# Attention output with the values stationary in 32 columns per head, normalised between two block transposes

## The chip, the cores and the metric

The kernel runs on one core of a Trainium2 chip. A core has five engines that run their own instruction streams and wait for one another through semaphores: TensorE (PE, matrix products; its weight loads are shown apart as PEld), VectorE (DVE), ScalarE (ACT), GpSimd (POOL) and SyncE (SP, which here issues the DMA transfers). Matrix products write to PSUM, which has eight banks per partition; everything else is in SBUF. The metric is the device time of one execution in microseconds (us). A profile of one execution gives every instruction's start and length.

## The reference

One layer of cross-attention and one feed-forward layer, each behind a layer norm and with a residual, for 2 batches of 1024 tokens of 256 numbers, all in float32. The context has 77 keys per batch, and there are 16 heads of 16 dimensions:

```
q = layernorm(x) @ Wq + bq        k = ctx @ Wk + bk        v = ctx @ Wv + bv
att = softmax(0.25 * q k^T * mask - 1e10 * (1 - mask))     over the 77 keys, per head
x   = x + (att v) @ Wo + bo
t   = layernorm(x)
x   = x + layernorm(t + relu(t @ w1 + b1) @ w2 + b2) * gamma + beta
```

The feed-forward layer has 8 experts in the reference, but the routing weights are set to the constant row (1, 0, ..., 0), so that only expert 0 (256 to 1024 to 256) enters the output.

## The kernel before, in words

Tokens go in eight halves of 256, and a half is two tiles of 128 tokens; there are 16 tiles. The stages of several halves are emitted interleaved. Products that carry the weights keep float32's accuracy by splitting each operand into a high and a low part of type float32r and summing three products (`up` line 573, `dn` line 602, `pq` line 404, `px1` line 531). The products of the softmax's numerators with the values are plain float32 ones, and a float32 product is two passes on TensorE, each with its own weight load.

For one tile the attention runs like this:

- scores for four heads at a time on TensorE (line 433) and the mask's factor on VectorE (line 444), into `u`, 128 tokens by 16 x 77 numbers;
- the mask's bias on GpSimd (line 453), the maximum per head (line 458) and its subtraction (line 462) on VectorE;
- the 1232 columns (head, key) of `u` are cut into ten chunks of 128 (the last has 80), regardless of where heads end, and each chunk is turned by TensorE against an identity matrix (`s_turn`, line 469), four to a PSUM bank;
- ScalarE takes the exponential out of that bank into `pT` (`s_exp`, lines 477 and 480);
- ten output products (`s_out`, line 487): the turned chunk is stationary, and 68 columns stream past it: the values of four heads with a column of ones after each, laid out in `vb` so that the rows of a chunk meet their own head's values and zeros elsewhere. All ten sum into one PSUM bank `po`, tokens on partitions;
- the column of ones gives the sum per head; VectorE takes its reciprocal (line 499) and multiplies (line 501) into `o` (`s_norm`).

The layout `vb` is made at the start: the values with bias go to `v_sb` (line 311), and 25 small DMA transfers, issued on SP's queue, place the pieces of heads in their chunks (`v_place`, stage `vp`). Both buffers are filled by GpSimd first (lines 251 and 253).

For a half, `o` of the two tiles is turned on TensorE (`o_turn`, stage `pot`, line 515), split into high on ScalarE (`o_hi`, line 519) and low on VectorE (`o_lo`, line 523), and projected (`px1`).

The order is not written by hand: the class `Stages` holds each stage with its engine, an estimated length, what it needs, a rank, and the ring of buffers it takes from; `order()` is a list scheduling over these numbers, and the stages are emitted in the order that comes out. Each engine then works through its own stream in that order. So an estimated length or a ring that changes also moves other stages. PSUM's eight banks are shared out as scores 2, turned chunks 1, general 3, feed-forward 2.

Of the kernel before, what the change touches and what calls it, by code (L numbers as in the profile page):

```python
"""Cross-attention layer and feed-forward layer, each behind a layer norm, on one NeuronCore.

The reference sets the routing weights to the constant one-hot row (1, 0, ..., 0), so the output is
the one of expert 0: the router and the experts behind weight 0 do not enter it.

Matrix products keep float32's accuracy: an operand x is split exactly into hi + lo, where hi is x
rounded to float32r (12 significant bits) and lo = x - hi fits float32r as well, and a product is
hi*hi + hi*lo + lo*hi with float32 sums. The scores stack hi and lo along the contraction, the
products with the softmax's numerators are float32 ones.

Tokens go in halves of 256: token 256 h + 2 p + n is in partition p, tile n. The stages of three
halves are emitted interleaved, so that the tensor engine has the feed-forward layer of one half
to do while the softmax of the next one runs on the other engines.
"""
# [12 lines left out]
AF = mybir.ActivationFunctionType  # L27
# [25 lines left out]
class Stages:  # L53
    """Stages of the computation, each on one engine, and the order to emit them in.

    A stage has the engine, a weight (its length), the stages it needs, a rank (the lower, the more
    urgent), and, where it takes a buffer of a ring, the ring, its size and the buffer's last readers.
    """
# [7 lines left out]
    def hop(self, k, u):  # L66
        """From the end of a stage to the start of one that needs it"""
        if k[0] == u[0]:
            return 0.0
        return {"VP": 0.26, "SS": 0.15, "VV": 0.13, "SV": 0.15, "VG": 0.16, "VS": 0.13, "GV": 0.07, "QP": 2.2, "QS": 2.2, "QV": 2.2}.get(  # L70
            self.all[k]["eng"] + self.all[u]["eng"], 0.2
        )

    def order(self):
        """List scheduling: whenever an engine is free, its most urgent stage that can start."""
# [59 lines left out]
def chunk_heads(T):  # L135
    """Rows (head, key) in chunks of 128: first of four heads, its own heads from and to, its rows"""
    out = []
    for r0 in range(0, H * T, P):
        r1 = min(r0 + P, H * T)
        out.append((min(r0 // T, H - 4), r0 // T, (r1 - 1) // T + 1, r1 - r0))  # L140
    return out


@with_exitstack
def layer(ctx: ExitStack, tc: tile.TileContext, a: dict, out: bass.AP):
# [6 lines left out]
    heads = chunk_heads(T)  # L152
    NCH = len(heads)
# [26 lines left out]
    # the activation table, before the first loads are here  # L180
    warm = const([P, 1], "warm")
    # the tensor engine's clock likewise
    zero = const([P, 512], "zero", mybir.dt.bfloat16)
# [4 lines left out]
    def warm_up(i):  # L188
        pw = bank(ps_s, f"pw{i}")
        nc.tensor.matmul(pw, lhsT=zero[:, :P], rhs=zero, start=True, stop=True)  # L190
# [59 lines left out]
    vb = const([P, B, NCH, 4, D + 1], "vb")  # L250
    nc.gpsimd.memset(vb, 0.0)
    v_sb = const([T, B, H, D + 1], "v_sb")
    nc.gpsimd.memset(v_sb, 1.0)
# [56 lines left out]
    def v_bias(b):  # L310
        nc.vector.tensor_tensor(
            v_sb[:, b, :, :D],
# [5 lines left out]
    # the pieces of the heads in the chunks of 128 rows  # L318
    pieces = []
    for c, (h0, ha, hb, r) in enumerate(heads):  # L320
        for h in range(ha, hb):
            r0, r1 = max(h * T, c * P), min((h + 1) * T, c * P + r)
            pieces.append((c, h, h - h0, r0, r1))

    def v_place(c, h, k, r0, r1):
        load(vb[r0 - c * P : r1 - c * P, :, c, k], v_sb[r0 - h * T : r1 - h * T, :, h])

# [1 line left out]
    sts = {}  # L329

    def stats(src, name):
        """mean and variance + eps of tiles of tokens"""
# [64 lines left out]
    def a_query(h):  # L397
        # Group g = 2 c + j holds heads 4 g .. 4 g + 3: one half of the partitions hi, the other lo.
# [65 lines left out]
    def s_turn(h, n, s):  # L464
        uf = us[h, n].rearrange("p h t -> p (h t)")
        pt = pss["t", h, n, s] = bank(ps_t, f"pp{h}_{n}_{s}", (P, 4, P))
        for c in range(4 * s, min(4 * s + 4, NCH)):
            r = heads[c][3]
            nc.tensor.transpose(pt[:r, c - 4 * s], uf[:, c * P : c * P + r], ident)  # L469

    def s_exp(h, n, s):
        if s == 0:
            pTs[h, n] = work([P, NCH, P], "pT", f"pT{h}_{n}", RINGS["pT"])
        pT, pt = pTs[h, n], pss.pop(("t", h, n, s))
        c0, c1 = 4 * s, min(4 * s + 4, NCH)
        full = c1 if heads[c1 - 1][3] == P else c1 - 1
        nc.scalar.activation(pT[:, c0:full], pt[:, : full - c0], AF.Exp)  # L477
        if full < c1:
            r = heads[full][3]
            nc.scalar.activation(pT[:r, full], pt[:r, full - c0], AF.Exp)  # L480
# [351 lines left out]
```

## Time and profile before

| what | us |
|---|---|
| median of three runs (239.4 to 240.75) | 239.61 |
| span of the profiled execution, first to last instruction | 237.8 |
| TensorE busy / its weight loads | 217.8 / 205.7 |
| VectorE busy | 185.9 |
| GpSimd busy | 155.3 |
| ScalarE busy | 126.0 |

The profiled execution's own time is known by its span, 237.8 us; the median of the runs lies 1.8 us above it. In the lines of the profile, L487 is line 487 of the kernel, `out<-in` names the tiles, xN is a count, and "idle before" is time that the engine stood still ahead of that group, with what ended it. The slices cut the span into 40 equal parts and give the busy share of each in tenths. The chain is followed back from the last instruction to whatever released it, so that it names the work that set the end. Matmuls are pipelined and their ends are modelled, so the lengths of neighbouring matmuls overlap; the distance between starts is the better price.

### The profile page before, as it was taken

The numbers are of one execution on the slowest core, as the hardware profiler recorded it, in microseconds if no ns is written. First come the engines' busy times: TensorE is split into PE (matmuls) and PEld (weight loads), VectorE is DVE, ScalarE is ACT, GpSimd is POOL, SyncE is SP. The second block draws the span as 40 slices with busy tenths as digits, with TensorE's granted clock in tenths as the row PEclk, the third lists the DMA queues.
The fourth block names the chain that finished last, engine by engine and source line by source line (L and its number), as shares of the span: only waits on it lengthen the run. The fifth ranks groups of instructions, "written<-read, shape, count | busy, mean of one in ns | idle before, by whom it ended". The sixth has DMA issues, their size and how long they took to land.

```text
span 237.8 us, 4535 instructions
## 1 busy us (share of the span) xinstructions
PE 217.8 (92%) x1726; PEld 205.7 (86%) x1727; DVE 185.9 (78%) x385; ACT 126.0 (53%) x268; POOL 155.3 (65%) x131
## 2 busy tenths in 40 slices
PE   8799788799997899799999999999999999999980
PEld 3589567698996798799999999999999999999970
DVE  2378998999999999999987789997962473727544
ACT  2369952635573676564465737625375365274510
POOL 5048899976988468683728976668254557575641
PEclk9869958999999999999999999999999999999997
DMA  6991001500000000000000001000010001001011
GB/s 181 335 373 19 10 7 36 193 3 0 4 0 0 3 0 0 21 28 3 0 0 3 1 3 44 0 3 0 3 45 0 3 0 47 34 10 46 2 44 44
DMA packets 8875, 9.19 MB, mean 39 GB/s; under 512 B 3321, under 2 KB 6039, under 8 KB 8855
## 3 DMA queue, kind: packets, MB, share of 16 engines
q1 hardware_dynamic: 8855, 8.92, 11.7%
q8 instruction: 13, 0.21, 0.4%
q14 instruction: 7, 0.06, 0.1%
HBM read 6.65 MB, written 2.10 MB: 37 GB/s over the span
## 4 chain that ended last, share of the span: by engine, by line
PE 59%; DVE 30%; POOL 3%; ACT 2%; DMA 2%; issue 2%; SPq 0%; DVEq 0%
PE py L602 17%; PE pz L573 14%; PE po L487 8%; DVE u L444 5%; DVE u L462 5%; PE pp L469 5%; PE px L531 4%; DVE mx L458 3%; PE s L433 3%; DVE qs L422 3%; PE pq L404 3%; DMA wq<-in_L_xattn_Wq 2%; PE pk L290 2%; POOL w1l L266 2%; PE py L547 1%
## 5 line engine op out<-in xcount | busy, mean ns | idle before, releaser
L591 POOL TENSOR_TENSOR hl<-h,hh 128x512 fp32r<-128x512 f32 x32 | 42.7, 1337 | 25.1 <-ACT hh L587 24.0
L453 POOL TENSOR_TENSOR u<-u,mb 128x616 f32<-128x616 f32 x32 | 46.7, 1465 | 13.7 <-DVE u L444 10.1
L582 ACT ACTIVATE h<-pz,cols 128x256 f32<-128x256 f32 x64 | 26.8, 470 | 31.3 <-PE pz L573 30.2
L487 PE MATMUL po<-vb,pT 128*128 128x68 f32 (+1 forms) x320 | 41.1, 269 | 0.9 <-DVE o L501 0.7
L487 PEld LDWEIGHTS po<-vb,pT 128*128 128x128 f32 (+1 forms) x320 | 39.4, 191 | 1.5 <-DVE o L501 0.9
L477 ACT ACTIVATE pT<-pp 128x512 f32<-128x512 f32 (+1 forms) x48 | 23.4, 487 | 30.2 <-PE pp L469 29.9
L573 PE MATMUL pz<-yh,w1h 128*128 128x256 f32 x128 | 36.8, 287 | 0.0
L602 PE MATMUL py<-w2h,hh 128*128 128x256 f32 x128 | 36.5, 285 | 0.0
L573 PE MATMUL pz<-yl,w1h 128*128 128x256 f32 x128 | 35.7, 279 | 0.0
L573 PE MATMUL pz<-yh,w1l 128*128 128x256 f32 x128 | 35.7, 279 | 0.0
L602 PE MATMUL py<-w2l,hh 128*128 128x256 f32 x128 | 35.7, 279 | 0.0
L602 PE MATMUL py<-w2h,hl 128*128 128x256 f32 x128 | 35.7, 279 | 0.0
L444 DVE TENSOR_TENSOR u<-s,mk 128x308 f32<-128x308 f32 x64 | 28.0, 469 | 3.6 <-PE s L433 2.9
L433 PE MATMUL s<-kb,qs 128*128 128x308 f32 x128 | 28.1, 336 | 2.4 <-DVE u L444 2.2
L469 PE MATMUL pp<-ident,u 128*128 128x128 f32 (+1 forms) x160 | 25.9, 277 | 3.0 <-ACT pT L477 1.6
L462 DVE TENSOR_TENSOR u<-u,mx 128x1232 f32<-128x1232 f32 x16 | 27.9, 1744 | 0.1
L458 DVE TENSOR_REDUCE mx<-u 128x16 f32<-128x1232 f32 x16 | 22.8, 1426 | 2.2 <-POOL u L453 2.2
L587 ACT ACTIVATE hh<-h 128x512 fp32r<-128x512 f32 x32 | 20.2, 632 | 8.0 <-PE py L602 7.4
L602 PEld LDWEIGHTS py<-w2h,hh 128*128 128x128 f32 x128 | 24.2, 189 | 0.0
L602 PEld LDWEIGHTS py<-w2l,hh 128*128 128x128 f32 x128 | 24.1, 188 | 0.0
L573 PEld LDWEIGHTS pz<-yh,w1h 128*128 128x128 f32 x128 | 24.1, 188 | 0.0
L573 PEld LDWEIGHTS pz<-yl,w1h 128*128 128x128 f32 x128 | 24.1, 188 | 0.0
(92 smaller groups left out, 487.7 us busy)
## 6 DMA issues: line engine op xcount, KB each, us to landing
x<-in_x SPq DMA_DIRECT2D x8, 256.0 KB
wst<-in_L_ffn_w SPq DMA_DIRECT2D x8, 256.0 KB
out<-tg SPq DMA_DIRECT2D x7, 256.0 KB
rows<-in_rows SPq DMA_DIRECT2D x1, 640.0 KB
wk<-in_wk_twice SPq DMA_DIRECT2D x1, 512.0 KB
mk<-in_mask_1x1xSxS_fk SPq DMA_DIRECT2D x1, 308.0 KB
wq<-in_L_xattn_Wq SPq DMA_DIRECT2D x1, 256.0 KB
wv<-in_L_xattn_Wv SPq DMA_DIRECT2D x1, 256.0 KB
```

Source lines behind the costliest of these rows:

```text
L433: nc.tensor.matmul(sc[:, :W], lhsT=qs[h][g][:, n * P : (n + 1) * P], rhs=kb[b][j][:, g], start=(j == 0), stop=(j == 1),)
L444: nc.vector.tensor_tensor(us[h, n][:, 4 * g : 4 * g + 4], pss.pop((h, n, g))[:, :W].rearrange("p (h t) -> p h t", t=T), mk[:, h % HPB, n]. ...
L453: nc.gpsimd.tensor_tensor(v, v, mb[:, h % HPB, n].unsqueeze(1).to_broadcast([P, 8, T]), ALU.add)
L458: nc.vector.tensor_reduce(mx, u, AX.X, ALU.max)
L462: nc.vector.tensor_tensor(u, u, mxs.pop((h, n)).unsqueeze(2).to_broadcast([P, H, T]), ALU.subtract)
L469: nc.tensor.transpose(pt[:r, c - 4 * s], uf[:, c * P : c * P + r], ident)
L477: nc.scalar.activation(pT[:, c0:full], pt[:, : full - c0], AF.Exp)
L487: nc.tensor.matmul(pos[h, n][:, h0 * (D + 1) : (h0 + 4) * (D + 1)], lhsT=pTs[h, n][:r, c], rhs=vb[:r, h // HPB, c], start=(c == 0), stop=( ...
L573: nc.tensor.matmul(pz[:, i], lhsT=w[:, c, j * P : (j + 1) * P], rhs=v[:, c], start=(k == 0), stop=(k == 5))
L582: nc.scalar.activation(t[:, i], pz[:, i], AF.Relu, bias=b1[:, 2 * q + i : 2 * q + i + 1])
L591: nc.gpsimd.tensor_tensor(hl[h, q], hs.pop((h, q)), f(hh[h, q]), ALU.subtract)
L602: nc.tensor.matmul(pys[h, ns[0]][:, n], lhsT=v[h, q][:, i, n * P : (n + 1) * P], rhs=w[:, j], start=(q == 0 and n == ns[0] and i == 0 and ...
```

## The change

The values become the stationary operand and the turned scores the moving one. Each head is turned by itself (77 keys on the partitions, 16 transposes per tile, in four groups of four heads), and each head's values, 16 columns of values and 16 columns of ones, take 32 columns of the array; four heads go to the four column groups, so that their outputs lie on partitions 0 to 31, 32 to 63, 64 to 95 and 96 to 127. The output of a tile then has head dimensions on the partitions and tokens in blocks of 32 along the free side. VectorE transposes its 32 x 32 blocks, which puts tokens on the partitions and the sum beside the 16 values, takes the reciprocal, multiplies, and transposes the blocks back, which leaves `o` as the projection needs it. So the turn of `o` on TensorE goes, and the low part of `o` is made by GpSimd. The values need no placement by DMA any more: `vb` is filled with ones and the biased values are written into it. The planner gets new lengths for the stages, and the tile of zeros for the warm-up products is narrower and read repeatedly.

```diff
-    vb = const([P, B, NCH, 4, D + 1], "vb")
-    nc.gpsimd.memset(vb, 0.0)
-    v_sb = const([T, B, H, D + 1], "v_sb")
-    nc.gpsimd.memset(v_sb, 1.0)
+    vb = const([T, B, H, 2 * D], "vb")
+    nc.gpsimd.memset(vb, 1.0)
...
     def v_bias(b):
         nc.vector.tensor_tensor(
-            v_sb[:, b, :, :D],
+            vb[:, b, :, :D],
...
-    def v_place(c, h, k, r0, r1):
-        load(vb[r0 - c * P : r1 - c * P, :, c, k], v_sb[r0 - h * T : r1 - h * T, :, h])
...
+    def heads(i):
+        return [8 * (i // 2) + 2 * j + i % 2 for j in range(4)]
+
+    def s_turn(h, n, i):
+        pt = pss["t", h, n, i] = bank(ps_t, f"pp{h}_{n}_{i}", (P, 4, P))
+        for j, k in enumerate(heads(i)):
+            nc.tensor.transpose(pt[:T, j], us[h, n][:, k], ident)
+
+    def s_exp(h, n, i):
+        if i == 0:
+            pTs[h, n] = work([T, 4, 4, P], "pT", f"pT{h}_{n}", RINGS["pT"])
+        nc.scalar.activation(pTs[h, n][:, i], pss.pop(("t", h, n, i))[:T], AF.Exp)
+
+    def s_out(h, n, i):
+        if i == 0:
+            pos[h, n] = bank(ps_a, f"po{h}_{n}", (P, 2, 4, 2, 32))
+        for j, k in enumerate(heads(i)):
+            r = slice(32 * j, 32 * j + 32)
             nc.tensor.matmul(
-                pos[h, n][:, h0 * (D + 1) : (h0 + 4) * (D + 1)],
-                lhsT=pTs[h, n][:r, c],
-                rhs=vb[:r, h // HPB, c],
-                start=(c == 0),
-                stop=(c == NCH - 1),
+                pos[h, n][r, i // 2, :, i % 2],
+                lhsT=vb[:, h // HPB, k],
+                rhs=pTs[h, n][:, i, j].rearrange("k (b t) -> k b t", t=32),
+                start=True,
+                stop=True,
                 skip_group_check=True,
             )
 
     def s_norm(h, n):
...
+        ot = work([P, 16, 32], "ot", f"ot{h}_{n}", 1)
+        nc.vector.transpose(ot.rearrange("p b d -> p (b d)"), pos.pop((h, n)).rearrange("p c b e t -> p (c b e t)"))
+        rc = work([P, 16], "rc", f"rc{h}_{n}")
+        nc.vector.reciprocal(rc, ot[:, :, D])
+        on = work([P, 16, D], "on", f"on{h}_{n}", 1)
+        nc.vector.tensor_tensor(on, ot[:, :, :D], rc.unsqueeze(2).to_broadcast([P, 16, D]), ALU.mult)
+        if n == 0:
+            os[h] = work([P, 2, 2, P], "o", f"o{h}", 2)
+        nc.vector.transpose(os[h][:, n].rearrange("p c t -> p (c t)"), on.rearrange("p b d -> p (b d)"))
...
-    def o_turn(h):
...
-        nc.scalar.activation(oh[h], pss["o", h], AF.Copy)
+        nc.scalar.activation(oh[h], os[h], AF.Copy)
...
-        nc.vector.tensor_tensor(ol[h], pss.pop(("o", h)), f(oh[h]), ALU.subtract)
+        nc.gpsimd.tensor_tensor(ol[h], os.pop(h), f(oh[h]), ALU.subtract)
...
-                half("tr", "P", 0.435 * w, [("sb", n)], s_turn, n, s, lag=lag, ring=("t", BANKS["t"], [("ex", n, s)]))
+                half("tr", "P", 0.3, [("sb", n)], s_turn, n, i, lag=lag, ring=("t", BANKS["t"], [("ex", n, i)]))
...
-                    "po", "P", 0.8 * w, [("ex", n, s)] + ([("po", n, s - 1)] if s else []), s_out, n, s, lag=lag,
+                    "po", "P", 0.3, [("ex", n, i)] + ([("po", n, i - 1)] if i else []), s_out, n, i, lag=lag,
...
-            half("on", "V", 0.63, [("po", n, 2)], s_norm, n, lag=lag, ring=("o", 3, ["pot"]))
+            half("on", "V", 1.5, [("po", n, 3)], s_norm, n, lag=lag, ring=("o", 2, ["oh", "ol"]) if n == 0 else None)
...
-        half("pot", "P", 0.43, [("on", 0), ("on", 1)], o_turn, lag=lag, ring=("a", BANKS["a"], ["ol"]))
...
-        half("ol", "V", 0.6, ["oh"], o_lo, lag=lag)
+        half("ol", "G", 1.23, ["oh"], o_lo, lag=lag)
```

## The prediction

> **What bounds the kernel now.** I read the shares of the engines and the forty slices first, the chain that ended last second, stretches of the span third, and then the groups of instructions that the change touches.
>
> ```profile
> PE 217.8 (92%) x1726; PEld 205.7 (86%) x1727; DVE 185.9 (78%) x385; ACT 126.0 (53%) x268; POOL 155.3 (65%) x131
> PE   8799788799997899799999999999999999999980
> DVE  2378998999999999999987789997962473727544
> ```
>
> TensorE is busy nearly everywhere and VectorE is full from slice 4 to slice 20, so the average does not name one bound. The chain in order of time does:
>
> ```profile
> 79.41 2.17 DVE u L462
> 100.81 1.34 DVE mx L458
> 102.78 2.07 DVE u L462
> 104.98 0.63 PE pp L469 x4
> 115.23 0.44 PE pp L469 x4
> 117.83 0.84 PE po L487 x8
> 119.68 0.44 PE pot L515 x4
> 222.43 2.72 PE pz L573 x24
> ```
>
> To about 105 us it runs through VectorE (maxima and subtractions of the softmax), from there to the end through TensorE. The stretches agree: TensorE has idle time before 105 and none after.
>
> ```profile
> 20.00:40.00 20.00, 16.82 (x97) 14.05 (x96) 18.16 (x32) 13.39 (x28) 17.98 (x13) 0.83 0.09 9
> 40.00:60.00 20.00, 18.20 (x151) 17.04 (x150) 19.58 (x41) 9.48 (x23) 16.58 (x13) 1.00 0.22 67
> 60.00:80.00 20.00, 18.05 (x149) 17.15 (x149) 19.77 (x35) 11.50 (x24) 17.91 (x15) 1.00 0.01 2
> 80.00:105.00 25.00, 21.79 (x179) 20.48 (x177) 24.43 (x52) 15.42 (x34) 16.07 (x15) 1.00 0.03 11
> ```
>
> The columns after the length are TensorE, its weight loads, VectorE, ScalarE, GpSimd, clock. TensorE is idle for at least 3.2 + 1.8 + 1.9 + 3.2 = 10.1 us of these 85, VectorE for 3.1. The clock is 1.00 from 48 us on. So VectorE work added before 105 costs its full length, and TensorE work added after 105 does. Of 16 token tiles, 7 are subtracted (line 462) before 102 us and 9 after, so I put 7/16 of an edit in the first part and 9/16 in the second.
>
> ```profile
> L487 PE MATMUL po<-vb,pT 128*128 128x68 f32 x288 | 37.5, 268 | 0.9 <-DVE o L501 0.7 <-DVE yl L556 0.3
> L469 PE MATMUL pp<-ident,u 128*128 128x128 f32 x144 | 24.2, 277 | 3.0 <-ACT pT L477 1.6 <-ACT pT L480 0.6 <-POOL w1l L266 0.5
> L469 PE MATMUL pp<-ident,u 128*80 128x128 f32 x16 | 4.4, 273 | 0.0
> L501 DVE TENSOR_TENSOR o<-po,rc 128x256 f32<-128x256 f32 x16 | 6.8, 425 | 0.5
> L523 DVE TENSOR_TENSOR ol<-pot,oh 128x512 fp32r<-128x512 f32 x8 | 5.5, 687 | 0.9 <-ACT oh L519 0.9
> ```
>
> Busy times of matmuls overlap, so I price them by pitch in the chain: eight passes of po in 0.84, 0.105 each; four transposes in 0.44, 0.11 each. A po product is two passes (320 for 160 calls).
>
> **The change part by part.**
>
> Transposes of the scores. Ten chunks of 128 rows become 16 heads of 77: six more per tile. The 80-wide transpose takes 273 ns against 277 for 128, so the narrow side saves nothing; the 128 streamed columns set the pitch. 16 x 6 x 0.11 = +10.6 us of TensorE.
>
> Output products, removed: 320 x 0.105 = 33.6 us. Added: per tile 16 products of 128 streamed columns, two passes each, in 64 groups of four heads. A pass: the value projection streams 256 float32 columns with a pitch of 0.216 (unmerged starts 16.42, 16.64, 16.86, 17.07, 17.29, at full clock), so 128 columns take 0.108. The trace has no product in a quarter of the array's columns, so a group of four has bounds: 8 x 0.108 = 0.86 if nothing overlaps, 2 x 0.108 = 0.22 if all four run side by side. I take the middle, and why: the two passes of one product stand next to each other in the program and use the same columns, so the second waits for the first; if passes start in order, only the second pass of one head can run beside the first of the next. That is 5 steps, 0.54.
>
> The Trainium skill, "TensorE: Matmul & The Clock Gate", Part 3, "Measured speedup vs the span model", gives one matmul's length plus about 4 ns for each further tile, so a group by it would be an estimated 0.23 and the kernel near 239; its matmuls there are single ones, and the same part says that matmuls start and end in program order, which is against four at once when each product is a pair.
>
> Changing the array's shape. The only product of another shape is the 4-row bias of the keys (line 286), a 32-row tile:
>
> ```profile
> 16.42 1.24 PE L308 MATMUL pv<-wv,ct 128*77 128x256 f32 x5
> 17.59 0.29 PEld L286 LDWEIGHTS pk<-bk 4*128 4x128 f32 x2 [0.37 <-issue]
> 18.30 0.10 PEld L190 LDWEIGHTS <-zero 128*128 128x128 bf16 x1 [0.42 <-issue]
> ```
>
> The last pv pass starts at 17.29 and streams until 17.50; the bias load starts at 17.59. Its second pass starts at 17.96 and streams 308 columns until 18.22; the next full-shape load starts at 18.30. That is 0.09 lost on the way in and 0.09 on the way out, and the view names only "issue" for both, no wait on another engine. A first weight load without cover adds about 0.03 on each side (128 columns took 0.107 at 17.59; a quarter is 0.03). 0.24 a visit. In the changed program's order the groups form 57 visits: 13.7 us. Bounds: 0 and 13.7; I take 13.7, since both sides of the one case show it.
>
> So the products cost 64 x 0.54 + 13.7 = 48.3, which is +14.7. The four transposes of o per half (line 515) go: 8 x 0.44 = -3.5. TensorE in all: 14.7 + 10.6 - 3.5 = +21.8; 9/16 after 105 is +12.3. The other 9.5 before 105 lies in TensorE's 10.1 us of idle time and costs nothing; without that cover it would add up to 9.5.
>
> Normalising on VectorE. Now 0.25 + 0.425 = 0.68 per tile. Then: block transpose of 128x512 out of PSUM, reciprocal 0.25, product 0.425, block transpose of 128x256. The trace has no such transpose. Nearest rows of the sizes: 0.687 (line 523, 128x512 from PSUM) and 0.42 (statistics, 128x256): 1.78 per tile, +1.1. Bounds: the fastest row per element, the mask bias (128x616 in 0.470), gives 0.39 and 0.20, in all 1.27; the slowest, line 622 (0.689 for 256), gives 1.38 and 0.69, in all 2.75. The low part `ol` leaves VectorE, 0.69 per half, 3 of them before 105. First part: 7 x 1.1 - 2.1 = +5.7 (+2.0 to +12.4). After 105 VectorE is off the chain.
>
> The Trainium skill, "VectorE: DVE Perf Modes", "The three transpose paths", gives 311 ns for a 128x128 bf16 transpose on VectorE; if that grows with the columns, an estimate of 1.24 and 0.62 would make the first part +11 and the kernel about 262; no run here shows it.
>
> GpSimd takes `ol`: 8 x 1.34. Before 105 that is 3 x 1.34 = 4.0 against 16.5 idle; it is 0.65 longer on the path of a half, which other halves cover. ScalarE: four exponentials of 0.595 (2.38) for 1.73 per tile, +10.5 in all on an engine that is half idle. The `o` copy reads SBUF in place of PSUM, same size. The one transpose bank now makes four rounds per tile instead of three; the waits of line 469 for ScalarE were 2.2 us in the whole run, so one more round is under 1 us.
>
> Placement of the values. 25 issues on SP's queue go, with the waits behind them:
>
> ```profile
> 18.21 21.28 SPq L199 DMA_DIRECT2D vb<-v_sb  x25
> 39.56 2.35 PE L487 MATMUL po<-vb,pT 128*128 128x68 f32 x20
> ```
>
> The first output product starts at 39.56, when that queue is through; but it follows the transposes on TensorE without idle time, so I take 0. The other end: the first exponential ended at 37.83, so -1.7. The last weight chunk and four x loads are issued 21 us earlier; ScalarE's one wait of 2.4 for that chunk is off the chain. The vb and v_sb fills on GpSimd become one; nothing waits for them. The narrower zero tile changes nothing in size for the warm-up products.
>
> Order. The planner places 480 of 768 feed-forward matmuls before the last output product instead of 384, and none between tiles 5 and 8. TensorE may be starved there; 0 to 5 us, I take 0 because the sum for the first part already fills its idle time.
>
> Sum: +12.3 + 5.7 = +18.0 on a span of 237.8, 255.8. The median of the runs, 239.61, is 1.8 above that span: 257.6, say 257.
>
> **The rivals.** (1) Pairs overlap and the array changes shape for free: 64 x 0.54 - 33.6 + 7.1 = +8.1, 9/16 is 4.6, with 5.7: 250. For it: only one switch is seen in the trace. (2) Nothing overlaps: 68.8 - 33.6 + 7.1 = +42, +23.8 after 105; before it 18.5 do not fit in 10.1 + 5.7, so 8.4: 272. For it: nothing in the trace ever overlaps two matmuls. (3) Four really run side by side, with switches: 14.1 + 13.7 - 33.6 + 7.1 = +1.3; with VectorE 246. (4) Faster: four side by side, switches free. TensorE gets 12.4 shorter, 7.0 after 105, against 5.7: 238.3, and 234.6 with the cheap block transpose. It decides when a group including its switches costs under 0.26 us (VectorE at 5.7) or 0.36 (at 2.0). For it: the program puts the four outputs on separate quarters of the partitions, with nothing shared but the moving rows' partitions; against it: the pairs and the 0.09 gaps.
>
> **How the numbers follow.** My forecast 0.42 (own range 249 to 264, from VectorE's ends); rival 1 0.17; rival 2 0.12; rival 3 0.10; rival 4 0.15; 0.04 for others. The range 238 to 270 leaves out half of rival 4 and most of rival 2. A measurement here can tell 0.5%, 1.2 us. Rival 4 and part of the others give faster 0.17; same 0.05; slower 0.78.
>
> **What would show it.** Right: a pitch of about 0.11 between heads inside a group, gaps near 0.09 on both sides of each group, transposes 0.11 apart, TensorE on the chain after about 110, a block transpose of 0.6 to 0.7 us. Wrong: starts of four heads a few ns apart, no gaps, or transposes of heads under 0.1; or VectorE on the chain past 130 us.

## The result, and the profile after

The changed kernel takes 274.38 us (median of three runs, 274.29 to 275.93) against 239.61 before: 1.143 times as long, with a 95% interval from 1.135 to 1.150. The forecast was 257 with a range of 238 to 270. The sign was right; the size was 17 us short, and the time lies 4 us above the range. The profiled execution took 274.29 us with a span of 272.5, against 237.8 before: 34.7 us are to be found. Some runs of a kernel, at a lower granted clock, take over 1.5% longer than its fastest; the medians below are of all runs, the intervals of the ratios leave such runs out, and without them the medians of the experiments e1, e2, e5 and e18 would be 281.9, 276.9, 240.3 and 240.3.

First the engines' busy times and the slices of the changed kernel's page (digits are tenths of each of forty slices).

```profile
PE 236.9 (87%) x1983; PEld 199.1 (73%) x1983; DVE 207.0 (76%) x409; ACT 135.9 (50%) x268; POOL 166.0 (61%) x138
PE   8997788779999859987979999999999845999990
DVE  2599956889896999988988883899999875025255
PEclk9799757599999997999797999999999995999997
```

TensorE's share fell from 92% to 87%. It is no longer full behind the middle of the run: the slice at place 15 has a 5, those at 33 and 34 a 4 and a 5. In both places the chain that ended last runs through VectorE (92.5 to 101.1 us and 219.8 to 228.1 us). No engine became a bound that is always busy. The stretches say how much that is (columns after the length: TensorE, weight loads, VectorE, ScalarE, GpSimd, granted clock).

```profile
20.00:40.00 20.00, 16.37 (x110) 10.91 (x109) 16.59 (x27) 12.42 (x26) 18.56 (x13) 0.76 0.04 15
40.00:60.00 20.00, 15.04 (x110) 10.79 (x102) 16.21 (x30) 4.55 (x9) 9.80 (x7) 0.73 0.00 1
60.00:80.00 20.00, 18.66 (x172) 16.58 (x173) 18.80 (x48) 14.68 (x30) 17.29 (x15) 1.00 0.00 1
80.00:105.00 25.00, 20.88 (x172) 18.61 (x171) 22.58 (x41) 14.62 (x32) 18.64 (x16) 0.94 0.03 12
105.00:130.00 25.00, 22.82 (x236) 18.61 (x234) 22.48 (x38) 11.05 (x22) 8.72 (x7) 0.98 0.03 12
130.00:180.00 50.00, 47.26 (x419) 40.66 (x416) 40.27 (x74) 28.08 (x57) 37.55 (x28) 0.94 0.00 1
180.00:230.00 50.00, 41.66 (x399) 34.45 (x398) 44.27 (x82) 20.23 (x38) 25.80 (x21) 0.95 0.05 17
```

The last three in the old kernel:

```profile
105.00:130.00 25.00, 25.00 (x214) 24.69 (x215) 22.58 (x43) 12.99 (x29) 14.88 (x12) 1.00 0.01 1
130.00:180.00 50.00, 49.74 (x435) 49.51 (x435) 41.24 (x81) 28.91 (x65) 33.38 (x26) 1.00 0.03 12
180.00:230.00 50.00, 50.00 (x436) 50.00 (x435) 25.92 (x60) 24.23 (x51) 29.98 (x26) 1.00 0.06 22
```

Between 105 and 230 us TensorE stands idle for 2.2 + 2.7 + 8.3 = 13.2 us; in the old kernel it was 125.00 - 124.74 = 0.3. Before 105 its idle time is 3.6 + 5.0 + 1.3 + 4.1 = 14.0, where it was 10.1. The clock is lower as well: 0.76 and 0.73 in the first two stretches, where it was 0.83 and 1.00, and 0.94 to 0.98 in those from 80 to 230, where it was 1.00.

The chain that ended last, in order of time, shows what TensorE stands for. This is the changed kernel from 119.86 us on:

```profile
119.86 0.60 PE pp L448 x4
120.49 0.60 ACT pT L453
121.13 0.68 PE pp L448 x4
121.83 0.60 ACT pT L453
122.48 0.66 PE pp L448 x4
123.50 0.78 PE s L410 x4
...
126.16 0.60 ACT pT L453
126.89 0.65 PE pp L448 x4
127.56 0.60 ACT pT L453
128.21 0.66 PE pp L448 x4
128.87 1.34 PE po L461 x32
```

Four transposes, the exponential of that bank, the next four transposes into the same bank, and so on: each round takes 1.3 us, of which ScalarE has 0.60. In the old kernel's chain ScalarE does not appear here; between the transposes at 115.23 and those at 118.67 stood four score passes, twelve feed-forward passes and eight output passes. The rounds are the same; the filling between them is gone, and in this stretch TensorE stands four times for an exponential, 2.2 us in all. Its longest stand lies later. The chain comes to it through three more such rounds (215.33 to 219.25) and then runs on VectorE (short pieces left out):

```profile
219.78 0.73 DVE ot L473
220.82 1.04 DVE on L477
222.33 0.99 DVE tg L591 x2
223.32 1.27 issue
224.59 2.88 DVE tg L594 x2
227.47 0.61 DVE yl L525
228.12 10.34 PE pz L542 x71
```

Here TensorE waits 6.0 us for `yl`, the low part that its next feed-forward products need, while VectorE works through a tile's normalising and the end of a half's last layer norm. Some of the waits of the whole run (engine, line, waited for: sum, times, longest):

```profile
ACT pT L453 <- PE pp L448: 60.6, 45, 6.1
DVE x L505 <- PE px L500: 16.5, 3, 11.3
DVE tg L583 <- PE py L571: 9.9, 4, 4.8
PE s L410 <- DVE u L421: 7.6, 6, 3.1
PE pz L542 <- DVE yl L525: 6.9, 2, 6.0
DVE ot L473 <- PE po L461: 6.8, 7, 3.1
PE pp L448 <- ACT pT L453: 6.7, 12, 0.8
```

The exponential's wait for transposes doubled (29.9 before). TensorE's wait for `yl` is new; its 12 waits for exponentials were 4 before, 2.2 us in all; VectorE's 7 waits for output products, 6.8 us, were 0.4. Of TensorE's 13.2 idle us between 105 and 230, the exponentials make 4.0 and `yl` 6.0.

Now the parts that were priced one by one. A timeline of TensorE around one group of four heads (start, length, operation; starts in one row are merged, so the row says that eight passes start within it):

```profile
151.15 0.28 PE L542 MATMUL pz<-yh,w1l 128*128 128x256 f32 x1
151.35 0.43 PE L461 MATMUL po<-pT,vb 77*32 77x128 f32 x8
151.71 0.44 PE L448 MATMUL pp<-ident,u 128*77 128x128 f32 x2
```

All eight passes lie in 0.43 us, each of them about 0.28 to 0.3 long. Unmerged, four passes start at 151.355, 151.362, 151.368 and 151.375, and four more between 151.488 and 151.508. The records do not name head or pass; I read them as the first passes of the four heads and then their second ones. Four heads do run side by side, 7 ns apart. The Trainium skill, "TensorE: Matmul & The Clock Gate", Part 3, "Measured speedup vs the span model", has about 4 ns for each further tile, and that is near. The same part says that matmuls start and end in program order, and the forecast turned this against four at once; the trace shows four at once, so by this reading the second pass of a product does not hold back the first pass of the next head.

The groups of VectorE that are new or became slower (columns: count, then busy and the mean in ns of one, then idle time before):

```profile
L473 DVE STREAM_TRANSPOSE ot<-po 128x512 f32<-128x512 f32 x16 | 11.4, 712 | 7.0 <-PE po L461 6.8
L475 DVE RECIPROCAL rc<-ot 128x16 f32<-128x16 f32 x16 | 4.1, 253 | 0.5
L477 DVE TENSOR_TENSOR on<-ot,rc 128x256 f32<-128x256 f32 x16 | 10.9, 683 | 0.6
L481 DVE STREAM_TRANSPOSE o<-on 128x256 f32<-128x256 f32 x16 | 7.1, 445 | 0.6
```

A tile's normalising is 0.712 + 0.253 + 0.683 + 0.445 = 2.09 us.

### The profile page after: what moved, and what is told of

It is laid out like the page before. It is cut to its first block, busy times and chain, and to the rows that moved or that the text cites. A ratio compares the mean times of both kernels' runs of the same rounds, so it can differ in the third digit from the quotient of the medians.

```text
span 272.5 us, 5031 instructions
## 1 busy us (share of the span) xinstructions
PE 236.9 (87%) x1983; PEld 199.1 (73%) x1983; DVE 207.0 (76%) x409; ACT 135.9 (50%) x268; POOL 166.0 (61%) x138
## 4 chain that ended last, share of the span: by engine, by line
PE 62%; DVE 26%; ACT 7%; issue 3%; DMA 2%; POOL 1%; SPq 0%; ACTq 0%; DVEq 0%
PE py L571 14%; PE pz L542 13%; PE pp L448 11%; PE s L410 6%; PE po L461 6%; PE px L500 4%; PE pq L381 4%; DVE u L421 3%; ACT pT L453 3%; DVE tg L594 3%; DVE on L477 2%; DVE qs L399 2%; DVE u L439 2%; DVE ot L473 2%; DVE mx L435 2%
## 5 line engine op out<-in xcount | busy, mean ns | idle before, releaser
L453 ACT ACTIVATE pT<-pp 77x512 f32<-77x512 f32 x64 | 37.9, 592 | 61.3 <-PE pp L448 60.6
L560 POOL TENSOR_TENSOR hl<-h,hh 128x512 fp32r<-128x512 f32 x32 | 44.1, 1386 | 20.1 <-ACT hh L556 17.4
L448 PE MATMUL pp<-ident,u 128*77 128x128 f32 x256 | 44.2, 298 | 8.5 <-ACT pT L453 6.7
L448 PEld LDWEIGHTS pp<-ident,u 128*77 128x77 f32 x256 | 29.9, 154 | 21.4 <-issue 10.2
L542 PE MATMUL pz<-yl,w1h 128*128 128x256 f32 x128 | 37.7, 294 | 6.9 <-DVE yl L525 6.9
L410 PE MATMUL s<-kb,qs 128*128 128x308 f32 x128 | 33.0, 369 | 7.9 <-DVE u L421 7.6
L542 PE MATMUL pz<-yh,w1l 128*128 128x256 f32 x128 | 37.3, 291 | 0.0
L410 PEld LDWEIGHTS s<-kb,qs 128*128 128x128 f32 x128 | 21.6, 214 | 13.3 <-DVE u L421 10.2
L461 PE MATMUL po<-pT,vb 77*32 77x128 f32 x512 | 28.1, 300 | 1.0 <-ACT pT L453 1.0
L542 PEld LDWEIGHTS pz<-yh,w1l 128*128 128x128 f32 x128 | 25.5, 200 | 0.0
```

What stands on the lines that cost most here:

```text
L410: nc.tensor.matmul(sc[:, :W], lhsT=qs[h][g][:, n * P : (n + 1) * P], rhs=kb[b][j][:, g], start=(j == 0), stop=(j == 1),)
L448: nc.tensor.transpose(pt[:T, j], us[h, n][:, k], ident)
L453: nc.scalar.activation(pTs[h, n][:, i], pss.pop(("t", h, n, i))[:T], AF.Exp)
L461: nc.tensor.matmul(pos[h, n][r, i // 2, :, i % 2], lhsT=vb[:, h // HPB, k], rhs=pTs[h, n][:, i, j].rearrange("k (b t) -> k b t", t=32), st ...
L542: nc.tensor.matmul(pz[:, i], lhsT=w[:, c, j * P : (j + 1) * P], rhs=v[:, c], start=(k == 0), stop=(k == 5))
L560: nc.gpsimd.tensor_tensor(hl[h, q], hs.pop((h, q)), f(hh[h, q]), ALU.subtract)
```

## The experiments

All times are medians, single runs where they lie far apart; the old kernel was run beside each batch (239.1 to 240.2). "Above" is the difference to the old kernel of the same batch.

| work of the kernel | order of emission | us | above | ratio, 95% |
|---|---|---|---|---|
| new | old, stages moved at most ten places (e1) | 283.32 | 44.2 | 1.179 to 1.196 |
| old | new (e2) | 276.9 and 282.5 | 37.8 or more | |
| new | planner with measured lengths (e3) | 266.91 | 27.8 | 1.107 to 1.124 |
| new | searched for it (e4) | 258.08 | 18.6 | 1.073 to 1.081 |
| old | searched the same way (e5) | 240.64 | 1.1 | 0.999 to 1.007 |
| old, more VectorE work (e6) | old | 250.73 | 11.2 | 1.042 to 1.052 |
| old, a fourth round (e7) | old | 250.04 | 10.5 | 1.038 to 1.050 |
| old, both (e8) | old | 260.36 | 21.0 | 1.082 to 1.093 |
| new, `ol` on VectorE (e9) | as e1 | 283.38 | 44.1 | 1.175 to 1.192 |
| new, no reciprocal and product (e10) | as e4 | 253.14 | 13.8 | 1.052 to 1.062 |
| new, `ol` on VectorE (e11) | as e4 | 263.22 | 23.9 | 1.093 to 1.106 |
| new | as e1, normalising later (e12) | 270.16 | 30.0 | 1.116 to 1.130 |
| new, 56 zero products (e13) | as e4 | 266.77 | 26.6 | 1.100 to 1.118 |
| old, 24 zero products (e14) | old | 242.70 | 2.6 | 1.004 to 1.017 |
| new, two transpose banks (e15) | searched for it | 256.62 | 17.2 | 1.063 to 1.078 |
| new, three rounds (e16) | as e4 | 252.55 | 13.1 | 1.048 to 1.060 |
| new, three rounds, no reciprocal (e17) | as e4 | 250.65 | 11.2 | 1.040 to 1.052 |
| old, 77 rows of the array (e18) | old | 240.3 twice, 244.2, 247.0 | 0.6 or more | |

**Work or order?** The forecast took the order at nothing. So the two were parted: the new instructions in the old kernel's order, the old instructions in the new order, the new ones with the planner's lengths set to what the trace shows, and both kinds in orders searched with the measured durations. In e1, e2, e4, e5 and e7 to e17 a fixed list takes the place of the planner:

```diff
-        for key in st.order():
+        for key in map(stage, ORDER):
             st.all[key]["fn"]()
```

and in e3 four of the planner's lengths change:

```diff
-                half("tr", "P", 0.3, [("sb", n)], s_turn, n, i, lag=lag, ring=("t", BANKS["t"], [("ex", n, i)]))
+                half("tr", "P", 0.45, [("sb", n)], s_turn, n, i, lag=lag, ring=("t", BANKS["t"], [("ex", n, i)]))
...
-                    "ex", "S", 0.53, [("tr", n, i)] + ([("ex", n, i - 1)] if i else []), s_exp, n, i, lag=lag,
+                    "ex", "S", 0.6, [("tr", n, i)] + ([("ex", n, i - 1)] if i else []), s_exp, n, i, lag=lag,
...
-                    "po", "P", 0.3, [("ex", n, i)] + ([("po", n, i - 1)] if i else []), s_out, n, i, lag=lag,
+                    "po", "P", 0.46, [("ex", n, i)] + ([("po", n, i - 1)] if i else []), s_out, n, i, lag=lag,
...
-            half("on", "V", 1.5, [("po", n, 3)], s_norm, n, lag=lag, ring=("o", 2, ["oh", "ol"]) if n == 0 else None)
+            half("on", "V", 2.1, [("po", n, 3)], s_norm, n, lag=lag, ring=("o", 2, ["oh", "ol"]) if n == 0 else None)
```

> The changed kernel's instructions, all of them, emitted in the order that the planner gave for the kernel before: the fourth group of a tile (transposes, exponential, output products) is put beside the third, the turn of o is left out, 32 stages shift by at most ten places so that buffers come free. Theory order (the new work costs little, the planner's new order with its long stretches without feed-forward work starves TensorE): 238 to 250 us, TensorE's clock near 0.96. Theory work (VectorE's 2.09 us per tile for normalising instead of 0.68, and four rounds through one transpose bank, set the time in any order): 265 to 275 us. A value between splits the 35 us in that proportion.

> The kernel before's instructions, emitted in the changed kernel's order: the fourth group of a tile left out, the turn of o put ahead of its high part, the 25 placements of values behind the same weight load on SP's queue as before. The placements end near 39 us while the new order wants the first output product near 31, so up to 8 us may come from that alone. Theory order: 262 to 280 us. Theory work: 240 to 250 us.

> The changed kernel with the planner's lengths set to what its profile shows: four transposes 0.45 instead of 0.3, a group of output products 0.46 instead of 0.3, exponential 0.6 instead of 0.53, normalising 2.1 instead of 1.5. Nothing else. If the four lengths are what spoils the order: 245 to 258 us. If the order is spoilt by the start times and ranks that were found for other stages, or if it is not the order: 265 to 280 us.

> The changed kernel's instructions in an order searched for them: the planner with the lengths that the profile shows, and start times and ranks searched for these stages. Theory order (the 35 us come from an order that does not suit the new work): 235 to 252 us. Theory work: stays at 262 to 275 us.

> The kernel before's instructions, none changed, in an order searched in the same way. It says what the search itself is worth. If the order of before was near its best: 236 to 246 us. If there is as much to gain as the planner's lengths say: 225 to 233 us. The distance between this and the run before it is the price of the new work with orders of equal care: theory order 0 to 10 us, theory work over 20 us.

Neither simple theory stands. The old order does not rescue the new work: it is 9 us worse than the new one (283.32). The new order ruins the old work (276.92 in the faster of two runs), though not by the order alone: in e2's trace the 25 placements fill SP's queue from 18 us to 39.5, ScalarE waits 9.8 us for the weight chunk behind them, and TensorE's longest wait for an exponential is 9.6 us. Each order is bad for the other's work. With lengths as measured the planner gives 266.91, 7.5 less than the change as made; an order searched for the new work gives 258.08, 16.3 less. The same search finds nothing for the old work (240.64, level with 239.5). So with the same search for both, the new work costs 258.08 - 240.64 = 17.4 us (17.8 with 240.3), and the other half of the 34.8 is an order that does not suit it. Where that half lies, e4's stretches after 105 us show:

```profile
105.00:130.00 25.00, 24.98 (x249) 22.97 (x248) 23.20 (x48) 15.71 (x32) 19.61 (x16) 1.00 0.03 12
130.00:180.00 50.00, 49.05 (x472) 43.44 (x471) 46.08 (x87) 27.90 (x57) 37.17 (x29) 1.00 0.02 7
180.00:230.00 50.00, 48.62 (x463) 42.41 (x462) 44.19 (x82) 26.69 (x54) 31.92 (x26) 1.00 0.05 17
```

TensorE is idle for 125.00 - 122.65 = 2.4 us in place of 13.2, and the clock is 1.00. From the sixth tile's last output product to the ninth's the trace of the change as made has no feed-forward product, that of e4 has 156.

VectorE's waits in e1, the new work in the old order, show where an unfit order bites (kernel lines are some 55 higher where the list stands in the file):

```profile
DVE tg L638 <- PE py L626: 25.2, 6, 5.4
DVE ot L528 <- PE po L516: 19.6, 14, 4.1
```

VectorE reaches a tile's normalising 14 times before the tile's last product is done, and what is queued behind it stands. The old kernel had 0.4 us of this.

**What the pieces cost in the old order.** e6 gives the old kernel two idle block transposes per tile between the reciprocal and the product, e7 four more transposes and one exponential per tile through the one bank, e8 both.

```diff
+        for _ in range(2):
+            nc.vector.transpose(spare_to, spare)
```
```diff
+            half("tr", "P", 0.44, [("sb", n)], more_turn, n, 3, lag=lag, ring=("t", BANKS["t"], [("ex", n, 3)]))
+            half("ex", "S", 0.6, [("tr", n, 3), ("ex", n, 2)], more_exp, n, 3, lag=lag)
```

> The kernel before in its own order, with two more block transposes of 128x512 on VectorE between a tile's reciprocal and its product, about 1.4 us per tile, what normalising costs more in the changed kernel; they read and write spare tiles. Theory work, VectorE part: 7 tiles before 105 us cost 9.8 us and the rest little: 248 to 256 us. If a delay of 1.4 us in a tile is passed on to TensorE through an order that fits no more: 258 us or more. If neither: under 244 us.

> The kernel before in its own order, with a fourth round per tile through the one transpose bank: four more transposes of 77 columns and one more exponential of 77x512 ahead of the third group of output products, their results unused. TensorE gets 16 x 0.44 = 7.0 us more, 4 after 105 us. If only that counts: 243 to 248 us. If the round trip between TensorE and ScalarE stops TensorE (about 0.9 us per tile, 16 times): 252 to 262 us.

> The two additions of the runs before, together: two more block transposes on VectorE (11.2 us alone) and a fourth round through the transpose bank (10.5 us alone), in the kernel before and its order. If they add: 259 to 263 us, and about 22 us of the 44 that the new work costs in this order come from elsewhere (low part of o on GpSimd, the array's shape). If each makes the other worse, because a tile's delays lie one after another: 266 to 280 us.

The added block transposes took 0.683 us each, 21.9 in all, and cost 11.2: half. The forecast's rule for VectorE, 7 tiles of 16, would give 9.6, so that rule is near. The fourth round added 64 transposes, 7.0 us of TensorE; the same rule, 9/16, would give 3.9, and it cost 10.5. The other 6.6 I put down to the round trip; of it TensorE's waits for the added exponential show 3.6. The two pieces add up: 11.2 + 10.5 = 21.7 against 21.0 measured.

**The other half of the 44.** e9 takes the low part back from GpSimd, e12 moves each tile's normalising up to four places later in VectorE's order (three other stages move with it).

```diff
-        nc.gpsimd.tensor_tensor(ol[h], os.pop(h), f(oh[h]), ALU.subtract)
+        nc.vector.tensor_tensor(ol[h], os.pop(h), f(oh[h]), ALU.subtract)
```
```diff
-po.0.0.2 bi.1.1.0 mx.1.0 tr.0.1.0 po.0.0.3 on.0.0 sc.1.1.2 ex.0.1.0 sc.1.1.3 tr.0.1.1
+po.0.0.2 bi.1.1.0 mx.1.0 tr.0.1.0 po.0.0.3 sc.1.1.2 ex.0.1.0 sc.1.1.3 tr.0.1.1
...
+mu.1.1.3 fl.6 ex.0.1.2 ql.2.0 on.0.0 po.0.1.0
```

> The changed kernel in the order of before (283 us), with the low part of o computed by VectorE as before instead of GpSimd; nothing else. If GpSimd's 1.36 us in the path of each half, and what it takes from VectorE while both run, cost a good part: 265 to 276 us. If not: 280 to 288 us, since VectorE gets 0.69 us more per half.

> The changed kernel in the order of before (283 us), with each tile's normalising moved back by up to four stages in VectorE's stream, so that VectorE does other work until the fourth group of output products is there. In that run VectorE stood 19.6 us in front of the first block transpose, 14 times; in the kernel before it stood 0.4 in front of the reciprocal. If this standing is what remains of the 44 us beside the 22 of VectorE's work and the fourth round: 262 to 271 us. If it only moves elsewhere: 278 us or more.

GpSimd's low part is no cause (283.38 against 283.32). Moving the normalising gives 13.2 us back, and the wait that it was aimed at is gone from VectorE's list, which now begins so:

```profile
DVE tg L638 <- PE py L626: 23.5, 6, 5.5
DVE yl L580 <- ACT yh L575: 7.0, 2, 6.8
DVE x L560 <- PE px L555: 5.0, 3, 1.9
```

So the 44.2 of e1 are about 21 for the pieces of e8, 13 for VectorE standing in its queue, and some 10 that are left, if prices from the old kernel and from the new one may be added; no run tried that.

**What the 17 are made of in the new work's own order.** In e4's order: e10 without the reciprocal and the product, e11 with the low part on VectorE (the edit shown above), e16 without the fourth round, e17 without either. In an order searched anew: e15 with a second bank for the transposes and one general bank less.

```diff
-        rc = work([P, 16], "rc", f"rc{h}_{n}")
-        nc.vector.reciprocal(rc, ot[:, :, D])
-        on = work([P, 16, D], "on", f"on{h}_{n}", 1)
-        nc.vector.tensor_tensor(on, ot[:, :, :D], rc.unsqueeze(2).to_broadcast([P, 16, D]), ALU.mult)
```
```diff
     def s_turn(h, n, i):
+        if i == 3:
+            return
...
     def s_exp(h, n, i):
+        if i == 3:
+            return
...
-                rhs=pTs[h, n][:, i, j].rearrange("k (b t) -> k b t", t=32),
+                rhs=pTs[h, n][:, min(i, 2), j].rearrange("k (b t) -> k b t", t=32),
```
```diff
-BANKS = {'s': 2, 't': 1, 'a': 3, 'f': 2}
+BANKS = {'s': 2, 't': 2, 'a': 2, 'f': 2}
```

> The changed kernel in its own searched order (258 us), with the reciprocal and the product of the normalising left out: the second block transpose reads the first one's output. 0.93 us of VectorE less per tile, 15 us in all, so VectorE has about the load of before. If VectorE's load is the price of the new work in an order of its own: 243 to 251 us. If the price is TensorE's and its round trips with ScalarE: 255 us or more.

> The changed kernel in its own searched order (258 us), with the low part of o on VectorE instead of GpSimd. If GpSimd is the hindrance: 248 to 255 us. If VectorE's load is: 259 to 264 us, 0.69 us more for 8 halves.

> The kernel of 258.08 us without the fourth round of each tile: its four transposes and its exponential are left out, and the fourth group of heads multiplies the third group's numerators (part of the computation is left out). All else and the order stay. In the old kernel and order such a round, added, cost 10.5 us. If it is the price here too: 246 to 250. If a round that the order was searched for lies beside other work: 255 to 258.

> The kernel of 258.08 us without the fourth round, and without the reciprocal and the product on VectorE as well (both parts of the computation are left out). If the two prices add up, this is 5 us below the run without the fourth round, 241 to 245, and the old kernel's 239.6 is nearly reached: what is left is the block transposes and the array's switches. If they share one cover: within 2 us of the better of the two alone, 246 to 253.

> The new instructions in an order searched as for the kernel of 258.08 us, but with two banks for the transposed scores and two general ones (it had one and three), so that a tile's four rounds of transposes and exponentials need not wait for each other's bank. If the single bank is what keeps 12 of the 17 us: 246 to 252. If the bank is not the place, or the bank taken from the general ones costs as much as it gives: 256 to 262.

Reciprocal and product are worth 5 us, the fourth round 5.5, and both together 7.4: they share one cover. GpSimd is the better place for the low part by 5 us. e15 is 1.5 us faster than e4, and their intervals overlap. All the while 11.2 us stay above the old kernel when both pieces are gone, though e17 then has no more work on VectorE and TensorE than the old kernel in its searched order: VectorE is busy 193.4 us against 196.0, and on TensorE the 192 transposes are 32 more (3.5 us) where the turn of `o` (3.5) is gone. GpSimd has more, 172.9 us against 156.9, the low part among it; e11 took that part away and gave it to VectorE, so GpSimd's load by itself was not tested.

**The clock.** In e17 that remainder lies early. Its granted clock, and that of e5, in forty slices, e17 first:

```profile
PEclk9798555685999999999999999999999999999997
```

```profile
PEclk9889985899999999999999999999999999999996
```

By the stretches of the traces e17's clock is at half (0.51) from 23 to 47 and from 54 to 61 us, e5's (0.50) from 34 to 44. In all runs with the new work the mean clock was 0.90 to 0.956, in all runs of the old kernel and of e5 to e8 it was 0.95 to 0.98. It goes with the order as well: e2, the old work in the new order, had 0.88 and 0.909. Span times what the clock lacks of 1 is 18.6 us for e17 and 8.6 for e5, 10.0 apart, and the spans are 9.5 apart. That invites a conclusion, so it was tried: e13 puts zero products ahead of the early transposes of the new work, two for each set of four, e14 does the same to the old kernel as a control, and e18 lets the old kernel use only 77 rows of the array, as the new one does.

```diff
+    def keep_up(i):
+        pw = bank(ps_f, f"wk{i}")
+        nc.tensor.matmul(pw, lhsT=zero[:, :P], rhs=zero.unsqueeze(1).to_broadcast([P, 4, P]), start=True, stop=True)
```
```diff
-            r = heads[c][3]
+            r = min(heads[c][3], T)
             nc.tensor.transpose(pt[:r, c - 4 * s], uf[:, c * P : c * P + r], ident)
```

> The changed kernel in its own searched order (258 us), with two products of zeros, 0.21 us each at full clock, ahead of each group of transposes of the first seven tiles, 56 in all; they go to a feed-forward bank and nobody reads them. TensorE's clock was at half from 35 to 56 and from 66 to 73 us there. If the halved clock is a good part of the 18 us: the clock stays up and the time falls to 246 to 253 us. If not: 258 to 264 us, from 12 us of added work that partly fills waits.

> The control: the kernel before with the same products of zeros ahead of the transposes of its first four tiles, 24 in all. Its clock was at half from 21 to 28 and from 41 to 48 us only. If the clock counts there too: 236 to 238.5 us, which would be below both kernels; if VectorE's chain hides it: 239 to 242 us.

> The old kernel in its old order, with the same instructions, but the transposes of the scores, the exponentials and the output products use 77 of the array's 128 rows and columns, as the new ones do (the other rows' part of the computation is left out, and the values' places hold ones where they held zeros). Pitches and order stay. In all runs with the new products the granted clock was 0.914 to 0.951, in all with the old ones in an order of their own 0.958 to 0.976, and the span times what is missing from 1 makes about 10 us between them. If the clock is granted by how much of the array is in use: a clock of 0.92 to 0.94, a stretch at half clock that lasts longer than the 6.8 us at 31 to 38 us, and 246 to 250 us. If it is granted by whether TensorE works at all: 0.96 to 0.97 and 239 to 241 us.

Two readings in these texts are wrong: by the traces the clock is at half in e4 from 25 to 45 and from 55 to 62 us (0.50 and 0.52), and in the old kernel from 30 to 37 (0.51). The zero products begin at 34 us in e13 and at 35 in e14, so they come late for a part of it; e13 still has 0.50 from 23 to 36 and 0.57 from 53 to 61.

e13 raised the clock (0.951 in its profile, 0.928 in e4) and was 8.7 us slower: two zero products take 0.61 and one 0.38, a pitch of 0.23, so 56 are 13 us, and 4 came back, by the clock or because products fell into waits. The control paid 2.6 for 24 products (5.5 us), so 3 came back there, where far less of the clock was lacking. e18 gave 240.3 twice and 244.2 and 247.0 once each, so it shows no effect of the rows that the clock could explain, though it is too spread to exclude one of a few us. One measure is the old kernel itself: over 44 of its runs beside these batches the clock went from 0.95 to 0.98 by itself, and a microsecond more of what the clock lacks went with 0.34 us more span (correlation 0.73). By that, the 10 us that separate e17 from e5 in clock are worth 3 to 4 us of time. But what a low clock costs depends on where it falls, and in e17 the chain that ended last runs through TensorE there (start, length):

```profile
31.97 2.94 PE pq L436 x12
```

Twelve such passes took 1.42 in the old kernel's chain at 143.93, with the clock at 1.00. Over TensorE's pieces of that chain, length times what the clock lacks of 1 is 11.1 us in e17, 5.0 in e5 and 3.4 in the old kernel. So I estimate 3 to 6 us of the remainder for the clock; no run sets it apart.

What stays open is 4 to 7 us of the 17. One suspect was not tried: e16 and e17 keep an order that was searched for work that they no longer do.

## Why the prediction was wrong in size

- **"Order. ... 0 to 5 us, I take 0 because the sum for the first part already fills its idle time."** This step failed, and it is the largest: 16.3 us by e4. The text had seen the hole (480 feed-forward products ahead of the last output product, none between tiles 5 and 8) and priced it by the idle time of the first part. The harm is done after 105 us, where the forecast had TensorE full: 13.2 us of idle time, and 2.4 in e4's order. In the hole itself, 119.86 to 128.21, TensorE has no feed-forward products at hand and stands 2.2 us for exponentials (4.0 by 230 us). The largest stand, 6.0 us near its end, is for VectorE's chain; what the hole has to do with that one is not shown.
- **"After 105 VectorE is off the chain."** Failed. After 105 us VectorE's pieces make 30.5 us of the chain, 7.0 before. "VectorE on the chain past 130 us" was the forecast's own sign of being wrong, and it is there, at 174 to 188 and 219.8 to 228.1 us.
- **"The clock is 1.00 from 48 us on."** The sum took the old kernel's clock over without a term. Over the span, what the clock lacks of 1 makes 22.0 us in the changed kernel and 8.3 before; on TensorE's pieces of the chain it is 15.1 and 3.4. By this estimate up to 12 of the 34.7 us go with the clock, as a part of what order and work cost and not beside it; no run sets it apart.
- **Products of four heads, 48.3 us.** Too high. A visit was to cost 0.54 + 0.24 = 0.78. Measured over the 52 visits of one group, from the start of the pass before to the start of the second pass after, it is 0.737; less the two ordinary steps of 0.118 and 0.109 that leaves 0.51. The switches were right: the first pass starts 0.209 after the pass before it and the next work 0.203 after the last, where 0.118 and 0.11 are usual, so 0.09 each way, and the second pass after the group comes 0.172 behind the first, where 0.109 is usual, so 0.06 for a load without cover: 0.24 as forecast. The term that failed is the group itself, 0.27 for 0.54; its lower bound of 0.22, not the middle, was near (rival 3). A further group in the same visit costs 0.22 (0.777 - 0.557 in the fastest visits), so all are 57 x 0.51 + 7 x 0.22 = 30.6, which is 3.0 less than the old products, not 14.7 more.
- **Transposes, +10.6.** Right: 256 at 0.109.
- **TensorE in all, +21.8.** At full clock it is -3.0 + 10.5 - 3.5 = +4.0; that the busy time rose by 19.1 is in good part the lower clock (22.0 us lacking over the span against 8.3). Rival 2 came nearest with 272, but by luck: nothing in the trace bears out its sum.
- **Normalising, 1.78 per tile.** 2.09. The block transposes were close (0.712 and 0.445 for 0.687 and 0.42). The term that failed is the product, taken over at 0.425 and 0.683 in fact (the last section shows why). The Trainium skill, "VectorE: DVE Perf Modes", "The three transpose paths", scaled by columns, gave the estimate of 1.24 and 0.62: too slow by 1.7 and 1.4 times.
- **"One more round is under 1 us."** Failed in the old order. A round cost 10.5 there (e7) and 5.5 in the new one (e16), with its transposes, which the forecast priced apart; by its rule they are 9/16 of 7.0, 3.9, so the round trip is left with 6.6 and 1.6. The price was read from TensorE's waits for ScalarE, 2.2 us in the whole run. They were small because other products stood between the rounds; a fourth round lengthens each tile's path by 1.3 us.
- **The shares 7/16 and 9/16.** The first was near in e6, 9.6 for 11.2. With the measured sizes the forecast's own sum would be 9/16 of 4.0 for TensorE and 7 x (2.09 - 0.68) - 2.1 = 7.8 for VectorE, 237.8 + 10.0 + 1.8 = 250 us in all: further off than 257. That 257 is nearer is luck: a term 1.6 times too high hid a part of what the order and the round cost.
- **GpSimd's `ol` and the placement at 0.** `ol` is right by e9 and e11. The placement was not tried by itself; e2's trace shows that it can cost in another order.

## What to carry to other kernels

Where queues are filled in an order planned beforehand, a change of the work is also a change of the order, and both have to be priced: run the new work in the old order and the old work in the new one before believing either. Ahead of a run, look at what the plan puts between two rounds that go to and fro between engines through one buffer; if nothing stands there, the engine stands for the round trip, however small the waits of before were. Follow the chain of the other engine too: here the longest single stand of TensorE, 6.0 us, was for VectorE. And mend the planner's lengths first: here four numbers were worth 7.5 us of 35.

## What the hardware showed that was not expected

A product on VectorE whose two operands both lie in the on-chip memory stretches when a GpSimd instruction is under way as it starts. `on`, 128x256, took 424 to 426 ns in eight cases out of sixteen: in six GpSimd stood, in one its instruction ended 0.03 us after `on` began, in one it began 0.14 later. In the other eight `on` took 515 to 1424 ns and ended 0.28 to 0.29 us after the end of the GpSimd instruction that it had met. Its predecessor `o`, one operand from the accumulators in PSUM, took 424 to 427 in all sixteen, in eleven of them with GpSimd at work beside it. The worst case in the changed kernel's timeline (start, length):

```profile
90.39 1.29 POOL L528 TENSOR_TENSOR tg<-tg,rows 128x512 f32<-128x512 f32 x1 [0.70 <-PE py L516]
90.54 1.42 DVE L477 TENSOR_TENSOR on<-ot,rc 128x256 f32<-128x256 f32 x1
```

VectorE's product starts 0.15 after GpSimd's addition and ends 0.28 after that one's end, as if it had waited for it. The Trainium skill, "Trainium Architecture — The Big Picture", "What this means for kernel authors", says that the pair of ports which VectorE and GpSimd share is an exclusive lock, and these rows agree.

The two passes of one float32 product do not keep other products out, by the reading above: passes of four products in four column groups start 7 ns apart, and the four second passes follow 0.133 later. A group of eight passes of 128 columns then takes 0.51 us with both changes of the array's shape, and 0.22 without.
